# A graph layer on one core: edge matmuls on several partition bases, x in table order, spills by block, and the output's x part made ahead

## The chip, the core and the metric

The kernel runs on one core of a Trainium2 chip. The core has five engines that run side by side: TensorE (PE, with PEld for its weight loads), VectorE (DVE), ScalarE (ACT), GpSimd (POOL) and SyncE (SP). SP and ACT also issue ordinary DMA transfers, and POOL issues indirect ones (gathers). The metric is the time on the device in microseconds, from the first to the last instruction of a launch and what lies around it. The median of three runs before the change is 4903.21 us (4901.36 to 4903.9).

## The reference

There are 12,500 nodes with 96 features and 412,500 edges, sorted by destination; each has 4 attributes. Cut to what matters:

```python
def _mlp(h, W, b, gamma, beta):
    h = relu(h @ W + b)
    mu, var = mean(h, axis=0), mean(square(h - mu), axis=0)   # over all rows
    return gamma * (h - mu) * rsqrt(var + EPS) + beta

node_feat = _mlp(x, W_node, ...)                       # [12500, 96]
edge_feat = _mlp(edge_attr, W_edge, ...)               # [412500, 96]
message = concatenate([x[src], x[dst], edge_feat], 1)  # [412500, 288]
message = _mlp(message, W_msg, ...)
agg = segment_sum(message, dst, 12500)
out = layernorm(x + agg + node_feat)                   # each row
```

The three normalisations run over all nodes or all edges, so that the edge statistics must be complete before the first message can be formed, and the message statistics before the first output row.

## The kernel before

All numbers are float32. The message matmul is split: the products of x with the source part and with the destination part of W_msg are tables in DRAM, p_tab and q_tab, with a row for each node. Edges are worked in groups of 512 (GE), made of four tiles of 128 (GT = 4); four groups are a block (BG = 4). There are 806 groups and 202 blocks (NBL).

**Start.** `load_x` (L132) brings x, transposed to [96, 12544], in seven pieces on SP and ACT. `table` (L139) makes p_tab: one matmul for each of 98 blocks of 128 nodes, four to a PSUM tile, copies on DVE and ACT in turn, and a write for each four. Beside it, DVE computes each edge's place relative to its group's first destination (L163).

**Gathers.** `gather` (L261) issues one indirect DMA for each 128 edges; it brings 128 rows of p_tab by source (3223 in all). The first 104 groups (SPILL) are gathered and written to the DRAM tensor `spill` by SP (L272), group by group. The next 34 groups fill a ring of 34 tiles (RING). After that a gather waits until the message loop has used a tile.

**Nodes.** `nodes` (L178) makes q_tab, with all of its writes on ACT, the node branch's statistics (L187 to L189), and x plus the node branch in `agg`, which it writes to the DRAM tensor `xn_d` (L198). Then the space of x is given up.

**Edge statistics.** `edge_norm` (L200) loads the destinations, subtracts and writes `rel_d` (L208 to L212, two pieces). For each block it multiplies the 20 rows of edge attributes (4 groups x 5, the fifth row being ones) by three 128-column slices of the block-diagonal matrix `wide` (L221), applies Relu on ACT (L224) and takes statistics on DVE (L226). The attributes come from ACT's queue, four blocks to a load (J = 4), in three buffers.

**Messages.** The loop goes through the blocks in an order that mixes the 26 spilled blocks evenly among the others. `load` (L296) brings a block's attributes, relative destinations and rows of q_tab on SP. `prepare` (L310) makes four matmuls with 24 rows each (L316): the attributes and the relative destinations against `we`, whose four copies stand at different rows and are zero elsewhere. `message` (L320) multiplies per 128 edges (L324), adds the gathered rows (L330) and applies Relu (L331). `reduce` (L333) sums by destination with a matmul (L339) and adds to `agg` (L342) and to a Gram matrix for the message statistics (L343). `fetch` (L354) brings a spilled block back.

**Output.** After the message statistics, each block of 128 nodes gets two matmuls (L570 for the messages, L571 for the part from `xn_d`), statistics per row (L577, L578) and the scaling (L582), and is written out by SP (L585). `general` (L396) is for other inputs and isn't run here.

**What sets the order.** The source is traced once, and the framework's planner puts the instructions on the engines' queues. Among those whose inputs and buffers are there, by its own costs, it takes the one that comes first in the source; a later one can be placed ahead where an earlier one isn't ready. Each queue then runs strictly in that order. The transfers that SP and ACT issue take one of eight semaphores in turn, and a transfer waits for the one that had its semaphore before, whichever queue issued it. A pool that is opened after another has been closed takes its space, and waits for the tiles that lay there.

Of the kernel before, what the change touches and what calls it, by code (L numbers as in the profile page):

```python
# [22 lines left out]
P = 128  # L23
# [10 lines left out]
ER_ROWS = BG * (EK + 1)  # L34
# [6 lines left out]
NBK = 4  # L41

# [6 lines left out]
RING = 34  # L49
J = 4  # L50
# [14 lines left out]
def gnn(ctx, tc, t):  # L65
# [5 lines left out]
    xn_d = dram.tile([C, NN], F32, name="xn_d")  # L71
# [4 lines left out]
    vec = const.tile([C, len(_VECS)], F32, name="vec")  # L76
    w_node = const.tile([C, C], F32, name="w_node")
    w_msg = const.tile([C, 3, C], F32, name="w_msg")
    b_msg = const.tile([1, C], F32, name="b_msg")
    src = const.tile([P, NTP], I32, name="src")  # L80
    nc.sync.dma_start(w_msg, t["L0_gnn_W_msg"].rearrange("(s k) f -> k s f", k=C))
    nc.scalar.dma_start(src, t["src"])
    nc.scalar.dma_start(w_node, t["L0_gnn_W_node"])
    nc.scalar.dma_start(b_msg, t["L0_gnn_b_msg"])
    for i, name in enumerate(_VECS):
        nc.scalar.dma_start(vec[:, i:i + 1], t[name])
    v = {name[7:]: vec[:, i:i + 1] for i, name in enumerate(_VECS)}
# [10 lines left out]
    wide = const.tile([BG * EK, BG * C], F32, name="wide")  # L98
    we = const.tile([ER_ROWS, BG, C + WN], F32, name="we")
    step = const.tile([1, 2, WN], F32, name="step")  # L100
# [5 lines left out]
    for i in range(BG):  # L106
        k = EK * i
        for to in (wide[:, i * C:(i + 1) * C], we[:BG * EK, i, :C]):
            nc.scalar.dma_start(to[k:k + ED, :], t["L0_gnn_W_edge"])
            nc.scalar.dma_start(to[k + ED:k + EK, :], t["L0_gnn_b_edge"])  # L110
        nc.scalar.dma_start(we[k + ED:k + EK, i, C:], step[:, 0, :])
        nc.scalar.dma_start(we[BG * EK + i:BG * EK + i + 1, i, C:], step[:, 1, :])

    agg = const.tile([C + 1, NN], F32, name="agg")
    rel = const.tile([P, NGP, GT], F32, name="rel")
    base = const.tile([1, NGP], I32, name="base")
    mstat = const.tile([C, 2], F32, name="mstat")
    flag = const.tile([1, 1], I32, name="flag")
    nc.scalar.dma_start(base, t["base"])
# [12 lines left out]
    def load_x(pool):  # L132
        xt = pool.tile([C, NN], F32, name="xt")
        step = 14 * P
        for i, c in enumerate(range(0, NN, step)):
            (nc.sync if i % 2 == 0 else nc.scalar).dma_start(xt[:, c:c + step], t["x"][:, c:c + step])
        return xt

    def table(out, w, xt, work, ps, other=nc.sync):  # L139
        rows = out.rearrange("(b p) f -> p b f", p=P)  # L140
        for i in range(0, NB, NBK):
            n = min(NBK, NB - i)
            pt = ps.tile([P, NBK, C], F32, name="pt", bufs=3)
            for g in range(n):
                nc.tensor.matmul(pt[:, g, :], xt[:, (i + g) * P:(i + g + 1) * P], w, start=True, stop=True)  # L145
            r = work.tile([P, NBK, C], F32, name="trow", bufs=4)
            if (i // NBK) % 2:
                nc.scalar.activation(r[:, :n, :], pt[:, :n, :], AF.Copy)
            else:
                nc.vector.tensor_copy(r[:, :n, :], pt[:, :n, :])  # L150
            (other if (i // NBK) % 2 else nc.scalar).dma_start(rows[:, i:i + n, :], r[:, :n, :])

    rpool, xpool = ExitStack(), ExitStack()
    ring = rpool.enter_context(tc.tile_pool(name="ring", bufs=RING))
    xt = load_x(xpool.enter_context(tc.tile_pool(name="x", bufs=1)))
    with tc.tile_pool(name="win", bufs=1) as win, tc.tile_pool(name="win_w", bufs=2) as work, \
            tc.tile_pool(name="win_ps", bufs=2, space=PSUM) as ps:
        table(p_tab, w_msg[:, 0, :], xt, work, ps)
# [19 lines left out]
    def nodes(xt):  # L178

        with tc.tile_pool(name="nd", bufs=1) as one, tc.tile_pool(name="nd_w", bufs=2) as work, \  # L180
                tc.tile_pool(name="nd_ps", bufs=2, space=PSUM) as ps:
            table(q_tab, w_msg[:, 1, :], xt, work, ps, nc.scalar)
            stats = one.tile([C, -(-N // GE), 6], F32, name="nstats")
            for i, c in enumerate(range(0, N, GE)):
                n = min(GE, N - c)
                pn = ps.tile([C, GE], F32, name="pn")
                nc.tensor.matmul(pn[:, :n], w_node, xt[:, c:c + n], start=True, stop=True)  # L187
                nc.scalar.activation(agg[:C, c:c + n], pn[:, :n], AF.Relu, bias=v["b_node"], scale=1.0)
                nc.vector.bn_stats(stats[:, i, :], agg[:C, c:c + n])  # L189
# [4 lines left out]
            for c in range(0, NN, NN // 7):  # L194
                x, y = agg[:C, c:c + NN // 7], xt[:, c:c + NN // 7]
                nc.vector.scalar_tensor_tensor(x, x, a_n, y, op0=OP.mult, op1=OP.add)
                nc.vector.tensor_scalar(x, x, c_n, None, op0=OP.add)
                nc.scalar.dma_start(xn_d[:, c:c + NN // 7], x)  # L198

    def edge_norm():  # L200

        with tc.tile_pool(name="es", bufs=2) as work, tc.tile_pool(name="es1", bufs=1) as one, \
# [3 lines left out]
            for i in range(0, RW // GE, BG):  # L206
                lin = one.tile([EP // RW, BG, GE], I32, name="lin")
                nc.scalar.dma_start(lin, t["dlin"].rearrange("o (p g e) -> (o p) g e", g=RW // GE, e=GE)[:, i:i + BG, :])  # L208
                rlin = one.tile([EP // RW, BG, GE], F32, name="rlin")
                nc.vector.tensor_tensor(rlin, lin, first[:, i:i + BG].unsqueeze(2)  # L210
                                        .to_broadcast([EP // RW, BG, GE]), op=OP.subtract)
                nc.scalar.dma_start(rel_d.rearrange("o (p g e) -> (o p) g e", g=RW // GE, e=GE)[:, i:i + BG, :], rlin)  # L212
            stats = one.tile([P, NS, NBL, 6], F32, name="estats")
            for b in range(NBL):
                if b % J == 0:
                    ea = work.tile([BG * EK, J, GE], F32, name="ea", bufs=3)
                    n = min(J, NBL - b)
                    nc.scalar.dma_start(ea[:, :n, :], t["ea"][:, b:b + n, :])
                pr = ps.tile([P, NS, GE], F32, name="pr")
                for i in range(NS):  # L220
                    nc.tensor.matmul(pr[:, i, :], wide[:, i * P:(i + 1) * P], ea[:, b % J, :],  # L221
                                     start=True, stop=True)
# [37 lines left out]
    def fast(ring, xt):  # L260
        def gather(g):  # L261
            pg = ring.tile([P, GT, C], F32, name="pg")
# [7 lines left out]
        for g in range(SPILL):  # L270
            pg = gather(g)
            nc.sync.dma_start(spill[g // BG, :, g % BG, :], pg.rearrange("p a b -> p (a b)"))  # L272
        got = {g: gather(g) for g in range(SPILL, SPILL + RING)}

        nodes(xt)
        xpool.close()
        w_e, bias = edge_norm()

        with tc.tile_pool(name="fix", bufs=1) as fix, tc.tile_pool(name="msg", bufs=2) as work, \
                tc.tile_pool(name="msg_ps", bufs=2, space=PSUM) as ps:  # L280
            nc.vector.memset(agg, 0.0)
# [14 lines left out]
            def load(s, b):  # L296

                n = min(BG, NG - b * BG)
                ea = work.tile([ER_ROWS, GE], F32, name="ea")
                nc.sync.dma_start(ea[:BG * EK, :], t["ea"][:, b, :])  # L300
                nc.sync.dma_start(ea[BG * EK:, :], rel_d[:, b * BG * GE:(b + 1) * BG * GE]
# [8 lines left out]
            def prepare(s, b, ea):  # L310
# [4 lines left out]
                for i in range(n):  # L315
                    nc.tensor.matmul(pr[:, i, :], we[:, i, :], ea, start=True, stop=True)  # L316
# [48 lines left out]
            for s, b in enumerate(order):  # L365
# [4 lines left out]
                for g in range(b * BG, min((b + 1) * BG, NG)):  # L370
# [8 lines left out]
                    if g >= SPILL and ahead < NG:  # L379
                        got[ahead] = gather(ahead)  # L380
                        ahead += 1
# [14 lines left out]
    def general(w_e, bias):  # L396

        with tc.tile_pool(name="gd", bufs=1, space=DRAM) as gd, tc.tile_pool(name="gfix", bufs=1) as fix, \
# [41 lines left out]
            def message(n, gathered, ea, dstf, to_spare, c, nt, rows, stat):  # L440
# [3 lines left out]
                nc.tensor.matmul(pr[:, :m], we[:EK, 0, :C], ea, start=True, stop=True)  # L444
# [100 lines left out]
    w_e, bias = fast(ring, xt)  # L545
# [6 lines left out]
    with tc.tile_pool(name="fin", bufs=2) as work, tc.tile_pool(name="fin_ps", bufs=2, space=PSUM) as ps:  # L552
# [5 lines left out]
        nc.tensor.matmul(pd, l, ident[:C, :C], start=True, stop=True)  # L558
# [4 lines left out]
        for i in range(0, NB, NBK):  # L563
            n = min(NBK, NB - i)
            xn = work.tile([C, NBK * P], F32, name="xn", bufs=4)
            nc.scalar.dma_start(xn[:, :n * P], xn_d[:, i * P:(i + n) * P])
            py = ps.tile([P, NBK, C], F32, name="py", bufs=3)
            for g in range(n):
                b = i + g
                nc.tensor.matmul(py[:, g, :], agg[:, b * P:(b + 1) * P], d, start=True, stop=False)  # L570
                nc.tensor.matmul(py[:, g, :], xn[:, g * P:(g + 1) * P], ident[:C, :C], start=False, stop=True)  # L571
            st = work.tile([P, NBK, 6], F32, name="st", bufs=3)
            mv = work.tile([P, NBK, 2], F32, name="mv", bufs=3)
            sd = work.tile([P, NBK], F32, name="sd", bufs=3)
            y = work.tile([P, NBK, C], F32, name="y", bufs=4)
            for g in range(n):
                nc.vector.bn_stats(st[:, g, :], py[:, g, :])  # L577
                nc.vector.bn_aggr(mv[:, g, :], st[:, g, :])  # L578
            nc.scalar.activation(sd[:, :n], mv[:, :n, 1], AF.Sqrt, bias=eps, scale=1.0)
            nc.vector.reciprocal(sd[:, :n], sd[:, :n])  # L580
            for g in range(n):
                nc.vector.tensor_scalar(y[:, g, :], py[:, g, :], mv[:, g, 0:1], sd[:, g:g + 1],  # L582
# [39 lines left out]
```

## Time and profile before

| | us |
|---|---|
| median of 3 runs | 4903.21 |
| profiled execution | 4900.82 |
| its span, first to last instruction | 4899.1 |
| PE busy | 4229.2 (86%) |
| POOL busy | 3056.8 (62%) |
| DVE busy | 1845.6 (38%) |
| ACT busy | 1122.1 (23%) |
| mean granted TensorE clock | 0.708 |

The page lists each group of instructions with its line, engine, operation, what it writes and reads, how many there were, the busy time with the mean of one in ns, and the engine's idle time just before them with what ended most of it. The waits list who waited for whom: the total in us, how often, and the longest. In the timeline each row is a start, a duration, the instruction, and in brackets the idle time before it. In the table of stages each row is a stretch in us from the start with its length, then the busy time of each engine with its number of instructions, the granted clock, the DMA engines' busy share and GB/s. A matmul in float32 shows as two records.

### The profile page before, as it was taken

What the parts mean: (1) busy time and instruction counts of PE and PEld (TensorE: products, weight loads), DVE (VectorE), ACT (ScalarE), POOL (GpSimd) and SP (SyncE); (2) the same over time, 40 slices, a digit from 0 to 9 for tenths busy, and PEclk for the clock granted to TensorE, in tenths of its full rate; (3) what the DMA queues carried; (4) which work ended last, traced back from release to release, by engine and by line L of the source; (5) the groups of instructions that cost most, each with busy time, mean ns of one, the idle gap of its engine ahead of it and who ended that gap; (6) DMA issues with size and microseconds to landing.
All of it is one profiled execution on the core that took longest, in us unless ns stands there. A gap on an engine that the chain in (4) does not pass through costs nothing. (4 is left out here: it accounts for less than half of the span.)

```text
span 4899.1 us, 53507 instructions
## 1 busy us (share of the span) xinstructions
PE 4229.2 (86%) x16561; PEld 2777.4 (57%) x16561; DVE 1845.6 (38%) x4481; ACT 1122.1 (23%) x1289; POOL 3056.8 (62%) x3231
## 2 busy tenths in 40 slices
PE   7226999999979998888888888888888888888988
PEld 6102333333337776666666666666666666666667
DVE  2313333333345553333333333333333333333335
ACT  1102222222223332222222222222222222222220
POOL 2777772000007777777777777777777777777771
PEclk9655555555559997777777777777777777777775
DMA  5333210000002222222222122222222212222113
GB/s 162 114 105 100 86 50 24 8 8 8 8 20 61 55 55 52 53 52 52 52 52 52 45 53 52 52 52 52 52 52 53 52 45 52 52 52 52 46 45 87
DMA packets 213517, 266.70 MB, mean 54 GB/s; under 512 B 134615, under 2 KB 148023, under 8 KB 211564
## 3 DMA queue, kind: packets, MB, share of 16 engines
q0 software_dynamic: 103136, 158.62, 13.5%
q1 hardware_dynamic: 83212, 72.27, 4.9%
q10 hardware_dynamic: 26876, 32.28, 2.2%
q8 instruction: 137, 2.24, 0.2%
q14 instruction: 156, 1.28, 0.1%
HBM read 221.54 MB, written 41.35 MB: 54 GB/s over the span
## 5 line engine op out<-in xcount | busy, mean ns | idle before, releaser
L265 POOL DMA_INDIRECT pg<-p_tab,src x3223 | 3055.9, 948 | 1737.9 <-issue 866.2
L339 PE MATMUL pa<-h 128*97 128x127 f32 x6446 | 1066.1, 320 | 287.2 <-ACT h L331 282.3
L324 PEld LDWEIGHTS z<-rhs,left 127*128 127x128 f32 x6446 | 1030.9, 239 | 467.2 <-issue 244.1
L221 PE MATMUL pr<-ea,wide 20*128 20x512 f32 x1212 | 1035.3, 1053 | 207.3 <-DMA ea<-in_ea 144.6
L324 PE MATMUL z<-rhs,left 127*128 127x96 f32 x6446 | 1136.4, 326 | 72.5 <-DVE hs L330 68.0
L339 PEld LDWEIGHTS pa<-h 128*97 128x97 f32 x6446 | 926.6, 201 | 313.3 <-ACT h L331 304.3
L316 PE MATMUL pr<-ea,we 24*126 24x512 f32 x1612 | 1057.3, 788 | 14.0 <-DVE left L318 11.7
L330 DVE TENSOR_TENSOR hs<-z,pg 128x384 f32<-128x384 f32 x702 | 391.0, 557 | 1610.2 <-DMA pg<-p_tab,src 1066.4
L331 ACT ACTIVATE h<-hs 128x384 f32<-128x384 f32 x806 | 420.7, 522 | 2093.7 <-DVE hs L330 1384.1
L221 PEld LDWEIGHTS pr<-ea,wide 20*128 20x128 f32 x1212 | 396.1, 327 | 845.3 <-issue 779.4
L226 DVE BATCH_NORM_STATS2 estats<-r 128x6 f32<-128x512 f32 x606 | 379.3, 682 | 644.0 <-ACT r L224 644.0
L316 PEld LDWEIGHTS pr<-ea,we 24*126 24x126 f32 x1612 | 338.5, 230 | 379.7 <-issue 326.1
L224 ACT ACTIVATE r<-pr 128x1536 f32<-128x1536 f32 x202 | 292.8, 1450 | 948.7 <-PE pr L221 880.4
L317 ACT ACTIVATE left<-pr 96x2048 f32<-96x2048 f32 x202 | 376.9, 1866 | 476.9 <-PE pr L316 476.5
L318 DVE TENSOR_SCALAR left<-pr 30x2048 f32<-30x2048 f32 x202 | 462.8, 2291 | 16.5 <-ACT left L317 10.2
L342 DVE TENSOR_TENSOR agg<-pa,agg 97x30 f32 x806 | 149.2, 185 | 265.6 <-PE pa L339 261.9
L326 DVE TENSOR_TENSOR h<-rel,iota 128x120 f32<-128x120 f32 x806 | 205.1, 275 | 2.2
L343 DVE TENSOR_TENSOR gram<-pa,gram 97x97 f32<-97x97 f32 x806 | 202.1, 251 | 0.0
L330 DVE TENSOR_TENSOR hs<-z,pb 128x384 f32<-128x384 f32 x104 | 57.7, 554 | 164.5 <-PE z L324 163.4
L145 PE MATMUL pt<-w_msg,xt 96*128 96x96 f32 x392 | 86.7, 420 | 35.1 <-DMA xt<-in_x 32.8
L145 PEld LDWEIGHTS pt<-w_msg,xt 96*128 96x128 f32 x392 | 86.8, 333 | 47.7 <-DMA xt<-in_x 21.5
L570 PE MATMUL py<-dm,agg 97*128 97x96 f32 x196 | 62.0, 422 | 1.8 <-DVE y L582 1.5
(90 smaller groups left out, 440.8 us busy)
## 6 DMA issues: line engine op xcount, KB each, us to landing
pg<-p_tab,src POOLq DMA_INDIRECT x3223, 2.4
spill<-pg SPq DMA_DIRECT2D x104, 192.0 KB
pb<-spill SPq DMA_DIRECT2D x26, 768.0 KB
rhs<-q_tab SPq DMA_DIRECT2D x806, 11.2 KB
ea<-in_ea SPq DMA_DIRECT2D x202, 40.0 KB
ea<-in_ea ACTq DMA_DIRECT2D x50, 160.0 KB
xn_d<-agg ACTq DMA_DIRECT2D x7, 672.0 KB
q_tab<-trow ACTq DMA_DIRECT2D x24, 192.0 KB
```

Of the source, the lines that this page charges most:

```text
L221: nc.tensor.matmul(pr[:, i, :], wide[:, i * P:(i + 1) * P], ea[:, b % J, :], start=True, stop=True)
L224: nc.scalar.activation(r, pr, AF.Relu)
L226: nc.vector.bn_stats(stats[:, i, b, :], r[:, i, :])
L265: nc.gpsimd.indirect_dma_start(out=pg[:, i, :], out_offset=None, in_=p_tab[:, :], in_offset=bass.IndirectOffsetOnAxis(ap=src[:, k:k + 1], ...
L316: nc.tensor.matmul(pr[:, i, :], we[:, i, :], ea, start=True, stop=True)
L317: nc.scalar.activation(x[:C, :n, :], pr[:C, :n, :], AF.Relu)
L318: nc.vector.tensor_scalar(x[C:C + WN, :n, :], pr[C:, :n, :], 0.0, None, op0=OP.is_equal)
L324: nc.tensor.matmul(z[:, i, :], left[s % 2][:KR, g % BG, i * P:(i + 1) * P], rhs[:KR, s % 2, g % BG, :], start=True, stop=True)
L326: nc.vector.tensor_tensor(h[:, :, C + 1:C + 1 + WN], rel[:, g, :].unsqueeze(2).to_broadcast([P, GT, WN]), iota[:, None, :].to_broadcast([P ...
L330: nc.vector.tensor_add(hs[:, :n, :], z[:, :n, :], pg[:, :n, :])
L331: nc.scalar.activation(h[:, :n, :C], hs[:, :n, :], AF.Relu)
L339: nc.tensor.matmul(pa[:, :C + 1 + WN], h[:r, i, :C + 1], h[:r, i, :C + 1 + WN], start=i == 0, stop=i == n - 1)
```

## The change

- **x in table order.** x is loaded first, from a second copy in DRAM (`xp`) whose columns are permuted so that partition p of the table's blocks holds nodes 98 p to 98 p + 97. A table write is then 14 blocks (CH) with 5,376 contiguous bytes per partition. The small loads of weights follow the table, on SP, and are fewer. The writes of both tables alternate between SP and ACT.
- **Spills by block.** Four groups are gathered into one stage tile (two of them) and written at once; the ring has 30 tiles.
- **Several partition bases.** `wide` has three slices at partitions 0, 32 and 64, each with the 10 rows that its 128 columns need; the attributes are loaded to the same partitions (three loads for eight blocks, J = 8, two buffers). In the message loop the four groups' attributes stand at partitions 0, 32, 64 and 96 (from `eaq`, padded to 128 rows), and each matmul takes 6 rows of its own base.
- **The output's x part made ahead by node.** `nodes` runs after `edge_norm`, loads x once more, forms x plus the node branch in place, multiplies each block by a centring matrix (identity less 1/96), and writes the result by node to `y0_d`. The message part is centred in its own small matrix. The output then adds the two, squares, sums, and scales, for eight blocks at a time.
- q_tab is made before the statistics. The index part of `edge_norm` comes in four pieces instead of two.

```diff
-RING = 34
-J = 4
+RING = 30
+J = 8
+    def table(out, w, work, ps):
+        rows = out.rearrange("(p b) f -> p b f", b=NB)
+        for c in range(0, NB, CH):
+            r = work.tile([P, CH, C], F32, name="trow", bufs=3)
+            for j, i in enumerate(range(0, CH, NBK)):
...
+            (nc.scalar if c // CH % 2 else nc.sync).dma_start(rows[:, c:c + CH, :], r)
+    for i in range(NS):
+        k, n = Q * i, C - Q * i
+        nc.sync.dma_start(wide[k:k + EK, :n], t["wb"][:, C - n:])
+        nc.sync.dma_start(wide[k + EK:k + 2 * EK, n:], t["wb"][:, :P - n])
...
     def nodes():
+            xt = one.tile([C, NN], F32, name="xt")
+            for c in range(0, NN, NN // 7):
+                nc.scalar.dma_start(xt[:, c:c + NN // 7], t["x"][:, c:c + NN // 7])
...
-                nc.vector.scalar_tensor_tensor(x, x, a_n, y, op0=OP.mult, op1=OP.add)
-                nc.vector.tensor_scalar(x, x, c_n, None, op0=OP.add)
-                nc.scalar.dma_start(xn_d[:, c:c + NN // 7], x)
+                nc.vector.scalar_tensor_tensor(y, x, a_n, y, op0=OP.mult, op1=OP.add)
+                nc.scalar.activation(y, y, AF.Identity, bias=c_n, scale=1.0)
+            nc.vector.memset(agg, 0.0)
+            for i in range(0, NB, NBY):
+                n = min(NBY, NB - i)
+                py = ps.tile([P, 2, GE], F32, name="py0")
+                for g in range(n):
+                    nc.tensor.matmul(py[:, g // NBK, g % NBK * C:(g % NBK + 1) * C],
+                                     xt[:, (i + g) * P:(i + g + 1) * P], center, start=True, stop=True)
...
+                nc.scalar.dma_start(y0_d[i // NBY][:, :n * C], y0.rearrange("p a b -> p (a b)")[:, :n * C])
     def edge_norm():
-            for i in range(0, RW // GE, BG):
+            for i in range(0, RW // GE, 2):
...
-                    ea = work.tile([BG * EK, J, GE], F32, name="ea", bufs=3)
+                    ea = work.tile([P, J, GE], F32, name="ea")
                     n = min(J, NBL - b)
-                    nc.scalar.dma_start(ea[:, :n, :], t["ea"][:, b:b + n, :])
+                    for i in range(NS):
+                        nc.scalar.dma_start(ea[Q * i:Q * i + 2 * EK, :n, :],
+                                            t["ea"][EK * i:EK * (i + 2), b:b + n, :])
                 pr = ps.tile([P, NS, GE], F32, name="pr")
                 for i in range(NS):
-                    nc.tensor.matmul(pr[:, i, :], wide[:, i * P:(i + 1) * P], ea[:, b % J, :],
-                                     start=True, stop=True)
+                    nc.tensor.matmul(pr[:, i, :], wide[Q * i:Q * i + 2 * EK, :],
+                                     ea[Q * i:Q * i + 2 * EK, b % J, :], start=True, stop=True)
     def fast(ring):
-        for g in range(SPILL):
-            pg = gather(g)
-            nc.sync.dma_start(spill[g // BG, :, g % BG, :], pg.rearrange("p a b -> p (a b)"))
-        got = {g: gather(g) for g in range(SPILL, SPILL + RING)}
-        nodes(xt)
+        for b in range(SPILL // BG):
+            pg = ring.tile([P, BG, GT, C], F32, name="stage", bufs=2)
+            for i in range(BG):
+                gather(b * BG + i, pg[:, i, :, :])
+            nc.sync.dma_start(spill[b], pg.rearrange("p g a c -> p g (a c)"))
+        got = {g: ahead_of(g) for g in range(SPILL, SPILL + RING)}
+        with tc.tile_pool(name="tab_w", bufs=1) as work, tc.tile_pool(name="tab_ps", bufs=2, space=PSUM) as ps:
+            table(q_tab, w_msg[:, 1, :], work, ps)
         xpool.close()
         w_e, bias = edge_norm()
+        nodes()
             def load(s, b):
-                nc.sync.dma_start(ea[:BG * EK, :], t["ea"][:, b, :])
-                nc.sync.dma_start(ea[BG * EK:, :], rel_d[:, b * BG * GE:(b + 1) * BG * GE]
+                nc.sync.dma_start(ea, t["eaq"][:, b, :])
+                nc.sync.dma_start(ea[EK:P:Q, :], rel_d[:, b * BG * GE:(b + 1) * BG * GE]
...
-                    nc.tensor.matmul(pr[:, i, :], we[:, i, :], ea, start=True, stop=True)
+                    nc.tensor.matmul(pr[:, i, :], we[Q * i:Q * i + EK + 1, :],
+                                     ea[Q * i:Q * i + EK + 1, :], start=True, stop=True)
...
+            y0 = work.tile([P, NBY, C], F32, name="y0", bufs=6)
+            nc.scalar.dma_start(y0[:, :n, :], y0_d[i // NBY][:, :n * C].rearrange("p (b f) -> p b f", f=C))
...
-                nc.tensor.matmul(py[:, g, :], agg[:, b * P:(b + 1) * P], d, start=True, stop=False)
-                nc.tensor.matmul(py[:, g, :], xn[:, g * P:(g + 1) * P], ident[:C, :C], start=False, stop=True)
+                nc.tensor.matmul(py[:, g // NBK, g % NBK * C:(g % NBK + 1) * C],
+                                 agg[:, (i + g) * P:(i + g + 1) * P], d, start=True, stop=True)
...
+                nc.vector.tensor_add(x, py[:, :, :NBK * C], x)
...
+            nc.scalar.activation(sq[:, :n, :], y0[:, :n, :], AF.Square)
+            nc.vector.tensor_reduce(sd[:, :n], sq[:, :n, :], axis=AX.X, op=OP.add)
+            nc.scalar.activation(sd[:, :n], sd[:, :n], AF.Sqrt, bias=eps, scale=1.0 / C)
             nc.vector.reciprocal(sd[:, :n], sd[:, :n])
+            nc.vector.tensor_tensor(y[:, :n, :], y0[:, :n, :], sd[:, :n].unsqueeze(2).to_broadcast([P, n, C]), op=OP.mult)
```

## The prediction

> **What bounds the kernel now.** I read the page's table of groups first, then the waits, then the timeline where the waits pointed, then the busy times of stages. The table alone misleads: PE is busiest (86%), POOL only 62%.
>
> ```profile
> L265 POOL DMA_INDIRECT pg<-p_tab,src x3223 | 3055.9, 948 | 1737.9 <-issue 866.2
> L221 PE MATMUL pr<-ea,wide 20*128 20x512 f32 x1212 | 1035.3, 1053 | 207.3 <-DMA ea<-in_ea 144.6
> L226 DVE BATCH_NORM_STATS2 estats<-r 128x6 f32<-128x512 f32 x606 | 379.3, 682 | 644.0 <-ACT r L224 644.0
> ```
>
> Of POOL's idle 1737.9 us, 866.2 are "issue": about 0.30 us after each gather. A gather thus takes 0.948 + 0.30 = 1.25 us of POOL whatever else happens, and 3223 of them about 4020 us. The waits say where the rest went:
>
> ```profile
> POOL pg L265 <- DVE hs L330: 679.6, 10, 672.8
> PE pr L221 <- DMA ea<-in_ea: 144.6, 1, 144.6
> SPq L272 <- DMA rel_d<-rlin: 36.6, 1, 36.6
> ```
>
> One wait of 672.8 us: the ring of gathered groups is full and the message loop has not begun. The timeline has both of its ends, and the stage table what lies between:
>
> ```profile
> 80.92 1.10 POOL L265 DMA_INDIRECT pg<-p_tab,src  x1 [79.34 <-issue]
> ...
> 1454.20 0.94 POOL L265 DMA_INDIRECT pg<-p_tab,src  x1 [672.75 <-DVE hs L330]
> ```
>
> ```profile
> core 0: us, PE busy (x) PEld busy (x) DVE busy (x) ACT busy (x) POOL busy (x), PEclk, DMA share, GB/s
> ...
> 407.00:1420.00 1013.00, 1003.88 (x1176) 384.46 (x1176) 377.74 (x597) 285.66 (x198) 283.05 (x300) 0.50 0.11 32
> 1420.00:1454.00 34.00, 11.41 (x25) 5.90 (x26) 20.39 (x28) 2.17 (x2) 0.00 (x0) 0.50 0.15 51
> 1454.00:4806.00 3352.00, 2977.93 (x14489) 2196.58 (x14487) 1301.62 (x3433) 789.11 (x1008) 2523.30 (x2671) 0.78 0.21 51
> 4806.00:4899.00 93.00, 84.79 (x394) 84.07 (x394) 57.47 (x320) 7.43 (x25) 0.00 (x0) 0.50 0.38 104
> ```
>
> From 1454 to 4806, 2671 gathers in 3352 us are 1.25 us each: POOL sets the message loop, and PE has 374 us to spare in it. From 407 to 1420 PE sets the edge statistics, always at clock 0.50. From 4806 PE sets the output. So the time is: first gather 80.9; 552 gathers until the ring is full at 781.5; the wait of 672.8; the other gathers; the output. What shortens POOL's start, its wait or the output counts in full, and nothing else does.
>
> **Parts that act on the start.** x is loaded first, and in larger table writes (14 node blocks, 5.4 KB a row piece, in place of 384 B). Before, PE stood still from 18 to 39 us because the last three x pieces were issued on ACT behind some forty small ones. The first 12 us moved 256 GB/s; 4.8 MB of x at about 220 take 22 us, faster than PE consumes: 98 blocks x 2 records x 0.2145 us (132 records in 28.3 us at 49 us) = 42 us. First piece at about 8 us, end of PE at 50, copy 0.6 and the last 0.7 MB write some 6: the first gather at about 58, **23 us** earlier. The small loads now go by SP after the table; before them nothing waits but the statistics, at 125 us. A bound: 50 (writes free) to 75 (writes queued behind small loads).
>
> **Spills by block.** 26 writes in place of 104, through two stage buffers; the ring keeps 30 tiles. A stage takes 16 x 1.27 = 20 us of gathers, its write some 10 us, so POOL doesn't wait unless a write is held over 10 us. Such holds exist: the third wait above is a spill behind a transfer it has no data from, because the framework gives transfers eight semaphores in turn and each waits for its predecessor's. Worth perhaps 2 x 30 us, but only taken from POOL's later wait, so nothing as long as that exceeds it. The ring is now full after 416 + 120 = 536 gathers: 58 + 536 x 1.269 (700.6 us / 552) = **738**.
>
> **Edge statistics.** Three matmuls a block, each with 20 rows at base 0, become three with 10 rows at bases 0, 32 and 64. The trace has no matmul away from base 0. Bounds of a block: 5.12 us as now (6 records x 0.853), if nothing overlaps; 1.95 us if DVE limits it (3 BATCH_NORM_STATS2 in 1.88 us, and ACT 1.45). The Trainium skill (TensorE: Matmul & The Clock Gate, "Measured speedup vs the span model") gives 3.07 times for four 32-row tiles at 512 columns; three tiles would then give near 1.9 us, DVE's bound. Against this stands the row: x1212 records for 606 matmuls. A float32 matmul is two records on the same rows; if matmuls start in program order (as that page also has it), the second record of one can overlap only the first of the next, so three of six are saved: 3 x 0.853 = 2.56 us at clock 0.50, which 20 active rows never left before. I take **2.6 us**, nearer to the row than to the rule: 525 us for 202 blocks; by the rule 394.
>
> The beginning: q_tab needs PE another 42 us and then xt's space is free: about 125 us, against 407 before, when node statistics, xn_d's transfers (203 to 258) and two index loads (DVE waited for them 111 us) came first. These loads remain, four of half size: they take some 60 us from DVE (half of 111, rounded up). Unhindered, the statistics end at 125 + 60 + 525 = 710. But ACT's loads of edge attributes, three for 8 blocks now, share the eight semaphores with the spills, and the spills end only at 58 + 416 x 1.274 + 12 = 600. If the planner placed the loads among the spills as if a block took 5.12 us, the statistics are held to that pace until 600: (600 - 125) / 5.12 = 93 blocks, and about 10 more by buffers that are ahead; the 60 us are then hidden. The other 99 take 257: end at **857**. I take this: the semaphores are seen to bind in the trace, and a planner that knows of the overlap is not.
>
> **Nodes behind the statistics.** Before, they lay beside the spills for nothing. Now, after the statistics: xt is loaded again, on ACT (4.8 MB, 24 us, into the space that the edge loads had), 25 matmuls keep pace (+6), DVE has the edge aggregates before it (16.6), norm 4, first SCALAR_TENSOR_TENSOR 2.1 and ACT 1.7, then 98 centred matmuls at 0.427 = 42 us, under which the copies, memset (10.5) and y0 writes lie. That is about 85; then one block is prepared as between 1440 and 1454: 15-20 us. From the statistics' end to the first message: **105 us** (34 before; 80 to 140). First message at 857 + 105 = 962. POOL's wait: 962 - 738 = 224 in place of 672.8: **449 us** saved.
>
> **Message loop.** POOL still needs 1.25 us a gather. Its edge matmuls on four bases save PE 2 to 3 us a block, which is worth nothing behind POOL. The loads grow from 40 to 256 KB: 44 MB more in 3350 us, 13 GB/s beside 51; DMA share 0.21 leaves room. Per block PE had 3352 / 202 = 16.6 us. Against the change speaks the Trainium skill (TensorEngine Tiling, "Key Properties"): changing the tiling mode drains the engine. No row shows a drain here; two per block at 0.2 us (1.053 for an isolated record less 0.853) would be 81 us of PE's spare 374: nothing, by POOL's row; 81 us if that cover were gone.
>
> **Output.** One matmul a block in place of two: 98 x 0.427 = 42 us, not 84. DVE per 8 blocks: sum, reduce and product at about 0.96 (384 elements took 0.557) and 0.18: 3.05 x 12.25 = 37, just hidden under PE. 9.6 MB in 50 us need a DMA share of 0.38 x 93 / 52 = 0.68. Square might need a table load (1.28) each time it alternates with Sqrt: 0 to 33 us; I take 0, since Copy, Relu and Sqrt make only two loads now. 93 becomes 52: **41 us** saved.
>
> **Sum.** 4899.1 - 23 - 449 - 41 = 4386 in the span. The profiled execution took 4900.8, the median of the runs is 4903.2, 4 above the span: **4390**. In short, it is 3529 + the end of the statistics.
>
> **Rivals.**
> Statistics not paced, or full overlap (0.29): end at 710, time 4243; with 1.95 us a block they end before 633, POOL never waits, and 4166 is the floor. For it: 8 semaphores and two buffers give lead. Against: the two records of a matmul.
> No overlap (0.12): the slices run one after another. End 125 + 60 + 1034 = 1219, paced up to 1310: 4752 to 4843. For it: no row of the trace shows any overlap.
> Slower, one mechanism (0.05): matmuls of 6 rows one after another leave the clock low in the message loop, and PE becomes its bound. Cold, a block costs 4 x 3.51 + 6.8 = 20.9 us, warm 11.5. With the first message at 1324, more than 17.4 us a block (mean clock under 0.69, now 0.78) makes it slower; at 0.60, 19.0 us, it is 5214. Against: PE that is behind runs 128-row matmuls densely, and in such stretches (1500 to 1550) the clock is 0.83 to 1.00. With overlap, even all cold costs 18.3 a block: +343 us, 4733.
>
> **Numbers.** Likeliest 0.52, own range 4290 to 4490; the rivals 0.29, 0.12, 0.05; 0.02 that gains and losses meet within 0.2%, about what this measurement can tell from no change. The range is 4165 to 4700, leaving out the last three. Faster 0.93, same 0.02, slower 0.05.
>
> **What will show it.** First gather near 58 us; ACT's edge loads waiting for spills until 600, then one block of statistics each 2.6 us (5.1: no overlap; 1.95: full); xt's load after the statistics; one POOL wait of some 224 us; 1.25 us a gather after it; an output of 52 us. The prediction is wrong if a block is not near 2.6, if q_tab's writes on SP get behind spills (xt's space would stay taken), or if gathers in the loop slow down.

## The result and the profile after

The changed kernel takes 4425.6 us (median of four runs, 4425.0 to 4427.5) where the kernel before, beside it, takes 4902.9 (4901.4 to 4903.9): a ratio of 0.903, with an interval of 0.901 to 0.904. Forecast were 4390, with a range of 4165 to 4700. The profiled span is 4423.6 us. The total came out within 1%, but by luck: two steps of the sum behind it were wrong by 80 and 73 us in opposite directions, and nearly cancelled.

The groups of the changed kernel, from the page: engine, tiles and shapes, number, then busy time and mean ns of one, then idle time before them.

```profile
L283 POOL DMA_INDIRECT pg<-p_tab,src x2807 | 2651.8, 945 | 1130.3 <-issue 681.4
L349 PE MATMUL z<-rhs,left 127*128 127x96 f32 x6446 | 1212.3, 337 | 253.0 <-DVE hs L355 244.0
L240 PE MATMUL pr<-ea,wide 10*128 10x512 f32 x1212 | 384.7, 1096 | 336.6 <-ACT r L243 245.2
L340 PE MATMUL pr<-ea,we 6*126 6x512 f32 x1612 | 585.9, 879 | 49.4 <-DVE left L343 35.2
```

The statistics' matmuls (L240) have the same 1212 records as before, but their union is busy for 384.7 us and no longer 1035.3. The mean of one record has even grown, to 1096 ns: the records lie on top of each other. Its idle time is put down to ACT's Relu, but that is ten waits, the longest 79.8 us, in which ACT itself was held, as the waits below show.

The waits of the changed kernel (total, times, longest, in us):

```profile
POOL pg L283 <- DVE hs L355: 278.7, 14, 274.8
ACT r L243 <- DMA spill<-stage: 162.6, 6, 80.4
DVE rlin L227 <- DMA lin<-in_dlin: 152.1, 4, 43.6
```

POOL's one wait is 274.8 us in place of 672.8. The other two lines are what still keeps the statistics back: spills, and four loads of indices, for three of which DVE waits over 40 us each.

The busy times of its stages, one row for each stretch, of which the second and third are parts of the first (time from, to, length, then busy time and instructions of PE, weight loads, DVE, ACT and POOL, the granted clock, DMA share and GB/s):

```profile
300.00:450.00 150.00, 50.42 (x156) 14.14 (x156) 52.26 (x85) 37.63 (x26) 113.73 (x120) 1.00 0.35 98
330.00:400.00 70.00, 45.39 (x144) 12.61 (x138) 42.72 (x71) 32.05 (x23) 52.93 (x57) 1.00 0.37 97
400.00:450.00 50.00, 0.00 (x0) 0.00 (x0) 0.00 (x0) 0.00 (x0) 37.81 (x41) 1.00 0.29 87
450.00:600.00 150.00, 56.99 (x183) 16.68 (x186) 55.91 (x92) 45.14 (x32) 113.27 (x121) 1.00 0.35 90
600.00:650.00 50.00, 50.00 (x168) 13.91 (x162) 49.39 (x82) 39.04 (x28) 37.76 (x40) 1.00 0.35 73
865.00:1001.00 136.00, 71.83 (x270) 54.33 (x270) 80.81 (x81) 32.00 (x36) 0.00 (x0) 0.69 0.29 89
1001.00:4372.00 3371.00, 2711.53 (x14491) 2137.02 (x14490) 1290.22 (x3434) 779.21 (x1008) 2538.57 (x2687) 0.76 0.25 65
4372.00:4423.00 51.00, 42.23 (x197) 41.89 (x196) 34.08 (x53) 14.13 (x26) 0.00 (x0) 0.50 0.63 180
```

One Relu on ACT is one block of statistics. Between 300 and 600 us there are 26 + 32 = 58, on the mean one each 5.2 us, but not at an even pace: between 330 and 400 us there are 23, and between 400 and 450 none. From 600 on there are 28 in 50 us, one each 1.8 us, with DVE full (49.39 of 50). The message loop makes 2687 gathers in 3371 us, 1.255 each, exactly as before. The output takes 51 us.

Single instructions of the changed kernel, in order of time (start, duration, then in brackets the idle time before it and what ended it):

```profile
53.50 1.10 POOL L283 DMA_INDIRECT stage<-p_tab,src  x1 [51.92 <-DMA p_tab<-trow]
...
122.31 1.02 DVE L143 COPY trow<-pt 128x384 f32<-128x384 f32 x2 [31.33 <-DMA q_tab<-trow]
...
281.73 1.45 ACT L243 ACTIVATE r<-pr 128x1536 f32<-128x1536 f32 x1 [138.08 <-issue]
...
462.91 2.79 ACT L243 ACTIVATE r<-pr 128x1536 f32<-128x1536 f32 x2 [80.40 <-DMA spill<-stage]
...
864.01 1.28 ACT L121 ACT_TABLE_LOAD   x1
...
884.95 0.29 ACT L121 ACTIVATE norm_edge<-eaggr,eps 96x1 f32<-96x1 f32 x1 [19.65 <-DVE eaggr L269]
885.66 0.15 DVE L124 TENSOR_TENSOR norm_edge<-norm_edge,eaggr 96x1 f32<-96x1 f32 x1
885.97 3.52 ACTq L187 DMA_DIRECT2D xt<-in_x  x7
...
935.46 10.51 DVE L203 MEMSET agg<- 97x12544 f32 x1 [2.56 <-DMA y_d<-y0s]
946.84 31.89 PE L208 MATMUL py<-center,xt 96*128 96x96 f32 x148 [10.16 <-DVE y0s L212]
992.61 2.09 PE L340 MATMUL pr<-ea,we 6*126 6x512 f32 x8 [13.89 <-DMA ea<-rel_d]
...
994.81 1.87 ACT L342 ACTIVATE left<-pr 96x2048 f32<-96x2048 f32 x1 [60.96 <-DMA rhs<-q_tab]
```

The first gather is at 53.5. In between, on SP's queue alone, a write of q_tab stands behind three spills until 117.4, and DVE waits 31.33 us for it:

```profile
77.20 40.05 SPq L295 DMA_DIRECT2D spill<-stage  x3
117.41 0.34 SPq L144 DMA_DIRECT2D q_tab<-trow  x1
```

The first Relu of the statistics starts only at 281.7. At 462.9 the Relus go on after a hold of 80.40 us that is put down to a spill: ACT has issued its next load of attributes only at 462.5. The last Relu has ended at 864, where ACT turns to the edge norm. The second load of x is issued at 886.0, 22 us later, and the centred matmuls that follow it stand still for 10.16 us behind the clearing of agg. The last two lines are the best measure of overlap in this trace: eight records of four matmuls on four bases take 2.09 us, where eight records one after another took 7.16 us before (L316). PE's ends are modelled, but ACT begins to read all four results at 994.81, 2.20 us after the first record began.

### The profile page after: what moved, and what is told of

It is laid out like the page before. It is cut to its first block, busy times and chain, and to the rows that moved or that the text cites. A ratio compares the mean times of both kernels' runs of the same rounds, so it can differ in the third digit from the quotient of the medians.

```text
span 4423.6 us, 52945 instructions
## 1 busy us (share of the span) xinstructions
PE 3295.7 (75%) x16561; PEld 2425.7 (55%) x16561; DVE 1806.7 (41%) x4225; ACT 1131.1 (26%) x1301; POOL 3050.1 (69%) x3231
## 5 line engine op out<-in xcount | busy, mean ns | idle before, releaser
L283 POOL DMA_INDIRECT pg<-p_tab,src x2807 | 2651.8, 945 | 1130.3 <-issue 681.4
L364 PE MATMUL pa<-h 128*97 128x127 f32 x6446 | 1154.3, 338 | 367.6 <-ACT h L356 350.5
L349 PE MATMUL z<-rhs,left 127*128 127x96 f32 x6446 | 1212.3, 337 | 253.0 <-DVE hs L355 244.0
L240 PE MATMUL pr<-ea,wide 10*128 10x512 f32 x1212 | 384.7, 1096 | 336.6 <-ACT r L243 245.2
L340 PE MATMUL pr<-ea,we 6*126 6x512 f32 x1612 | 585.9, 879 | 49.4 <-DVE left L343 35.2
L283 POOL DMA_INDIRECT stage<-p_tab,src x416 | 397.4, 955 | 178.4 <-issue 126.5
L240 PEld LDWEIGHTS pr<-ea,wide 10*128 10x128 f32 x1212 | 108.3, 307 | 611.6 <-ACT r L243 509.2
L340 PEld LDWEIGHTS pr<-ea,we 6*126 6x126 f32 x1612 | 147.2, 237 | 122.6 <-DVE left L343 58.7
L351 DVE TENSOR_TENSOR h<-rel,iota 128x120 f32<-128x120 f32 x806 | 204.8, 275 | 2.1
L139 PE MATMUL pt<-w_msg,xp 96*128 96x96 f32 x392 | 85.0, 422 | 32.8 <-DVE trow L143 26.4
L139 PEld LDWEIGHTS pt<-w_msg,xp 96*128 96x128 f32 x392 | 84.0, 332 | 33.6 <-DVE trow L143 26.8
```

Of the source, the lines that this page charges most:

```text
L240: nc.tensor.matmul(pr[:, i, :], wide[Q * i:Q * i + 2 * EK, :], ea[Q * i:Q * i + 2 * EK, b % J, :], start=True, stop=True)
L283: nc.gpsimd.indirect_dma_start(out=pg[:, i, :], out_offset=None, in_=p_tab[:, :], in_offset=bass.IndirectOffsetOnAxis(ap=src[:, k:k + 1], ...
L340: nc.tensor.matmul(pr[:, i, :], we[Q * i:Q * i + EK + 1, :], ea[Q * i:Q * i + EK + 1, :], start=True, stop=True)
L349: nc.tensor.matmul(z[:, i, :], left[s % 2][:KR, g % BG, i * P:(i + 1) * P], rhs[:KR, s % 2, g % BG, :], start=True, stop=True)
L351: nc.vector.tensor_tensor(h[:, :, C + 1:C + 1 + WN], rel[:, g, :].unsqueeze(2).to_broadcast([P, GT, WN]), iota[:, None, :].to_broadcast([P ...
L364: nc.tensor.matmul(pa[:, :C + 1 + WN], h[:r, i, :C + 1], h[:r, i, :C + 1 + WN], start=i == 0, stop=i == n - 1)
```

## Experiments

The experiments ran on two other chips, which agree with each other and differ from the first: there the kernel before takes 6222 us, and the changed kernel 5738.8 (ratio 0.922, 0.919 to 0.924). The saving, 484 us, is close to that of the first chip (477), but the kernel before was not traced on these chips, so it is not shown that it is made up in the same way. Expected totals that were written for a chip like the first are therefore read as differences, against 5738.8 or against the run beside it. The edits are shown shortened.

**The changed kernel again.**

> The changed kernel itself, as the measure for the runs beside it. On a chip like the first: 4425 us, statistics held until about 600 us and ended near 864, POOL's wait 275 us. On a chip as slow as that of the earlier experiments (before: 6222 us there), near the 5733 us of the run with the split index transfers, or up to 40 us more, since that run took away the waits for indices.

Measured: 5738.8 us, within what was expected for such a chip. Its timeline in the statistics, with POOL's gathers left out:

```profile
607.61 1.45 ACT L243 ACTIVATE r<-pr 128x1536 f32<-128x1536 f32 x1 [14.65 <-remote]
...
609.12 2.08 PE L240 MATMUL pr<-ea,wide 10*128 10x512 f32 x6 [14.02 <-issue]
...
624.41 1.45 ACT L243 ACTIVATE r<-pr 128x1536 f32<-128x1536 f32 x1 [15.35 <-remote]
```

While POOL gathers, a block of statistics comes each 16.80 us here: PE has its six records done at 611.2, and ACT reads them at 624.4, though it has been idle for 15.35 us and its operands are there. When POOL's ring is full, at about 800 us, a block takes 1.84 us at once. On the first chip POOL gathered on from 600 to 726 us and the blocks took 1.86 beside it. What holds ACT on these chips is not in the records, and it stays open. The message loop is slower too: from 1400 to 5600 us there are 2611 gathers, one each 1.61 us, and POOL, which on the first chip set that loop at 1.255, now waits for DVE in it (637.4 us for L351). Three things follow. What is gained under POOL's gathers can hardly show here, so three of the experiments below (the index transfers alone, the three holds, the spills on POOL) are inconclusive. What sets the loop on the first chip can't be tested here either. And an isolated block is seen: **six records on three bases in 2.08 us**, where three matmuls one after another would be 5.12.

**Statistics slices back on base 0** (20 rows in every slice, the attributes loaded to partitions 0 to 19 only, one tile less in the ring).

```
-  matmul(pr[:, i, :], wide[Q*i:Q*i + 2*EK, :], ea[Q*i:Q*i + 2*EK, b % J, :])
+  matmul(pr[:, i, :], wide[:, i*P:(i + 1)*P], ea[:BG*EK, b % J, :])
```

> The changed kernel with its statistics slices put back to partition base 0 (20 rows each, three loads kept; ring 29 for space). If the gain comes from matmuls on different bases overlapping: a block of statistics takes 5.1 us again, about 150 blocks are left at 600 us, the statistics end near 1370, POOL's wait grows to some 780 us and the time is near 4930. If the gain comes from the earlier start and the other parts: a block stays under 3 us and the time within 20 us of 4425.

Measured: 6291.1 us, 552 more than the changed kernel on such a chip, and 1.1% more than the kernel before beside it (ratio 1.0108, interval 1.009 to 1.013). A window of this kernel, then one of the changed kernel in the same stage, in the columns given above, and POOL's longest wait for each:

```profile
1000.00:1200.00 200.00, 200.00 (x236) 78.11 (x235) 73.29 (x117) 56.55 (x39) 0.00 (x0) 1.00 0.03 8
```

```profile
900.00:1000.00 100.00, 100.00 (x327) 27.91 (x324) 98.70 (x163) 78.31 (x55) 0.00 (x0) 1.00 0.15 34
```

```profile
POOL pg L280 <- DVE hs L352: 1121.1, 31, 1030.7
```

```profile
POOL pg L283 <- DVE hs L355: 567.8, 33, 479.3
```

39 blocks in 200 us are 5.13 us each, against 55 in 100 us, 1.82: PE full in the one, PE and DVE in the other. POOL's wait grows by 551 us, the time by 552. So the partition bases are what the statistics owe their speed to, and the whole of it goes through POOL's wait. Without them the rest of the change gains nothing here: its nodes now stand between the statistics and the first message. The clock is granted at 1.00 in both, and a record at base 0 still takes 200 / 236 = 0.85 us, as it did at 0.50 before, on the first chip. The granted clock is therefore not what made the statistics fast.

**Edge matmuls of the loop back on base 0** (24 rows, with loads of 40 KB in place of 256; two tiles less in the ring).

```
-  matmul(pr[:, i, :], we[Q*i:Q*i + EK + 1, :], ea[Q*i:Q*i + EK + 1, :])
+  matmul(pr[:, i, :], we0[:, i, :], ea[:BG*(EK + 1), :])
```

> The changed kernel with the message loop's edge matmuls put back to base 0 (24 rows, 40 KB loads; ring 28 for space). If POOL sets the loop: PE's busy time in it grows by some 470 us (586 to 1057 for these matmuls), a gather stays at 1.255 us, and the time is 4425 within 10 us. If the bases matter in the loop (PE's clock or its drains): at least 40 us away from 4425, either way.

Measured: 5712.5 us, 0.5% under the changed kernel. Its group of these matmuls:

```profile
L346 PE MATMUL pr<-ea,we 24*126 24x512 f32 x1612 | 927.9, 700 | 140.2 <-issue 110.0 <-DVE left L348 19.7 <-DMA ea<-in_ea 10.4
```

PE is 325 us busier with them (927.9 against 602.8 in the changed kernel there; 470 was expected), and the kernel isn't slower for it. On these chips the loop isn't set by POOL alone, so this does not yet show what the bases are worth on the first. There the two traces show it: in the loop PE was busy for 2977.93 us before and for 2711.53 after, and a gather took 1.255 us both times. So the four bases are worth nothing in the loop, as forecast. Of a drain at each change of tiling no row shows a sign: in the changed kernel's trace PE's idle time before these matmuls is 49.4 us, of which 35.2 are put down to DVE, so drains on the way into them could be 14 us at most, as far as they show as idle time. The 26 us that this kernel is faster may be theirs, or those of the smaller loads: the run doesn't part them.

**Index transfers cut at partition 96.**

```
-  dma_start(lin, dlin[:, i:i + 2, :])
+  for lo, hi in ((0, 96), (96, 101)):
+      dma_start(lin[lo:hi], dlin[lo:hi, i:i + 2, :])        # rel_d likewise
```

> The changed kernel with each index transfer of 101 partitions cut into 96 and 5. If these transfers run on one DMA engine and hold the statistics until 281 us: each load takes under 20 us instead of 44, DVE's wait for them falls from 152 us to under 60, the first Relu comes before 220 us, some 15 more blocks are done by 600, and the time is near 4397. If the spills alone set the pace: the waits shrink and the time stays at 4425 within 8 us.

Measured: 5733.2 us, no difference from 5738.8. The waits for the loads shrank as expected: those that DVE's index subtraction has put down to them fall from 64.8 us to 5.1 (and those put down to nothing that the profile shows from 87.5 to 44.5), and the first Relu comes at 239 us in place of 342. But after it the statistics crawl at 16.8 us a block until POOL stops, and the last Relu comes at 1126 in place of 1138. What the 103 us would be worth on a chip like the first, this run can't tell.

**One spill in place of 26** (`SPILL = BG`). POOL's ring is full at 229 us, and after that neither gathers nor spills are left to disturb the statistics.

> The changed kernel with one spilled block instead of 26: nothing else moves, but POOL fills its ring by about 230 us and waits long, so it is slower as a whole. If the spills hold the statistics through the shared semaphores: these run at 1.86 us a block as soon as the index loads are over, end near 665 us, and the time is 665 + 137 + 3087 gathers at 1.255 + 52, some 4730. If something else holds them: they still end near 864 and the time is near 4930.

Measured: 5801.9 us. With the spills gone the statistics still got going only at 403 us, after two blocks at 371; from there they took 1.85 us a block and ended at 782. q_tab's copies had crawled until POOL stopped, and were done at 266; from there to 400 the four loads of indices followed one another. One row of its stage table, in which DVE, ACT and POOL stand almost still:

```profile
300.00:350.00 50.00, 3.78 (x4) 1.16 (x4) 1.23 (x1) 0.00 (x0) 0.00 (x0) 1.00 0.07 27
```

The DMA share is 0.07 of 16 engines, about what one engine can fill (an estimate: 1/16 is 0.06). The run after this one tests whether the cut changes that.

**One spill, and index transfers cut.**

> One spill only, and the index transfers cut at partition 96. With one spill and whole transfers the gathers had stopped at 229 us, no spill was left, and still the statistics got going only at 403 us, DVE waiting 124 us for four loads of indices. My theory (a transfer over 101 partitions is slow, and ACT's queue holds the attribute loads behind it): the four waits fall from 35 us to under 10 us each, the statistics get going about 100 us earlier, near 300 us, end near 680 in place of 782, and POOL's wait falls from 695 to about 595 us; the time falls by about 100 us. Rival (the indices wait for another reason, the shared eight semaphores or the q_tab writes): the four waits stay over 25 us each, and nothing moves by more than 20 us.

Measured: 5676.8 us, 125 less. The waits of the run with one spill, then of this one:

```profile
DVE rlin L227 <- DMA lin<-in_dlin: 123.7, 4, 35.2
...
POOL pg L283 <- DVE hs L355: 698.5, 2, 695.0
```

```profile
DVE rlin L228 <- DMA lin<-in_dlin: 18.4, 4, 6.9
...
POOL pg L285 <- DVE hs L357: 587.4, 4, 580.2
```

The waits for indices fall from 124 to 18 us; the statistics run from 295 us on and end at 668 in place of 780; POOL's wait is 115 us less. That is the theory's result, and the rival's (nothing moves by 20 us) is out. Uncut, DVE waits some 35 us for three of the four loads of 404 KB over 101 partitions (43 on the first chip), and ACT's queue holds the attribute loads and the Relus behind them. Cut into 96 and 5, a load keeps DVE waiting for less than 7 us; between 279 and 285 us, in the midst of them, the DMA share is 0.70. Loads and writes of the indices were cut together, so that their parts are not told apart.

**xt loaded by SP.**

```
-  nc.scalar.dma_start(xt[:, c:c + NN // 7], x[:, c:c + NN // 7])
+  nc.sync.dma_start(xt[:, c:c + NN // 7], x[:, c:c + NN // 7])
```

It was tried twice: alone, and on top of one spill and cut index transfers, where q_tab's writes were also put on ACT alone.

> Only the second loading of xt is issued by SP in place of ACT. My theory (the load stood in ACT's queue behind the edge norm's chain with its Sqrt): the load is issued within 3 us of the statistics' end, not 22 us after it; the first message comes about 20 us earlier, POOL's wait is 275 - 20 = 255 us and the time is 20 us less than the changed kernel's on the same chip. Rival (the nodes' stage is set by its memset, its y0 copies and its centred matmuls, and the load was covered): 0 to 5 us less.

> One spill only, index transfers cut at partition 96, q_tab written by ACT alone, xt loaded by SP. Against the run with one spill and cut transfers: xt's load is issued when the last statistics are done, not behind the edge norm's Sqrt (24 us later in the run with one spill), so the first message comes about 20 us earlier and POOL's wait is about 20 us less; the time falls by another 20 us. Rival (the nodes' stage is set by what follows the load): the first message comes less than 6 us earlier.

Measured: 5730.0 us for the first (0.9205 of before, interval 0.918 to 0.923: no difference from 0.9218), and 5676.8 for the second, the same as with one spill and cut transfers only. My theory, that the load stood in ACT's queue behind the Sqrt, fell. The timelines of the run with one spill and cut transfers, where ACT issues the load, and of the second of these, where SP does:

```profile
690.08 0.15 DVE L124 TENSOR_TENSOR norm_edge<-norm_edge,eaggr 96x1 f32<-96x1 f32 x1
...
690.38 3.64 ACTq L187 DMA_DIRECT2D xt<-in_x  x7
```

```profile
683.97 0.15 DVE L124 TENSOR_TENSOR norm_edge<-norm_edge,eaggr 96x1 f32<-96x1 f32 x1
...
684.25 3.37 SPq L187 DMA_DIRECT2D xt<-in_x  x7
```

SP's own wait in this run:

```profile
SPq L187 <- DVE norm_edge L124: 36.2, 1, 36.2
```

On either queue the load is issued 0.13 to 0.15 us after L124 has ended, 22 us after the last Relu, and the first message comes 139 us after that Relu in both. L124 is the last instruction that reads eaggr, a tile of the edge norm's own; xt is given the space that these tiles hold. The changed kernel's timeline shows the same order: ACT has done its Sqrt at 885.24 and would have been free, L124 ends at 885.81, the load is issued at 885.97. So the queue is not what holds the load: it waits for L124 on either. That it does so for the space is read from the traces and the program; a kernel that gives xt space of its own was not tried.

**Three holds taken away together** (indices, q_tab's writes all on ACT, xt by SP), and **the same with the spills issued by POOL** through three stage buffers, the ring cut to 25.

```
-  nc.sync.dma_start(spill[b], pg)
+  if b: nc.gpsimd.dma_start(spill[b - 1], held)
+  held = pg
```

> Three holds taken away together: index transfers cut at partition 96, q_tab written by ACT alone, xt loaded by SP. If the late indices and q_tab are what kept the statistics to 57 blocks by 600 us, then about 100 are done by then, the statistics end near 780 instead of 864, and with 20 us of the nodes the time is 100 us less than the changed kernel's. Rival (the spills alone set the pace until 600, whatever comes before them): the statistics still end at 850 to 864, and the time is 20 to 35 us less.

> The same three, and the spills are issued by POOL one stage later, through three stage buffers (the ring has 25 tiles in place of 30). If the statistics were held because loads on ACT and spills on SP wait for one another in turn, then they run at 1.86 us a block from about 190 us on and end by 600; POOL's wait falls from 275 us to less than 40, and the time is near 4200 us on a chip like the first (4166 was the floor worked out). Rival (the loads are late for another reason, the planner's order or the transfers themselves): the statistics still end after 780 and the time is within 40 us of the run with three holds taken away.

Measured: 5723.8 (0.9194, interval 0.917 to 0.922) and 5737.4 us (0.9214). Neither can be told from 0.9218, and both expectations of a gain are missed. With the spills on POOL, POOL gathered without a pause (121 gathers from 150 to 300 us, against 96 in the changed kernel on this chip), and the other engines got less done beside it: PE 48 records in that time, against 136, and the first Relu at 573 us, against 342. The statistics again ran at 1.84 us only when POOL had stopped, and ended near 1130 us in both. On these chips that is the bound, so whether spills on another queue would free the statistics on a chip like the first was not shown.

## Why the prediction was right, step by step

- **First gather**: forecast 58, measured 53.5. Ring full: forecast 738, measured 727. Both from the first load of x and 1.25 to 1.27 us a gather.
- **A block of statistics: the step that failed first.** I took 2.6 us, arguing from the row that two records of one float32 matmul can't overlap and that only the second of one matmul with the first of the next could. From 600 us on it is 1.86 us on the first chip, DVE's bound. The isolated block settles why: six records in 2.08 us. One matmul's two records are 1.71, so the three run side by side almost from end to end; three of six records saved, as I had it, would have left 2.56. The clock, which I took to stay at 0.50, was granted at 1.00, but that made no record faster (slices back on base 0). The factor of 3.07 in the Trainium skill (TensorE: Matmul & The Clock Gate, "Measured speedup vs the span model") would have come nearer: an estimate from it for four matmuls is 4 x 1.71 / 3.07 = 2.2 us, and the four of the message loop took 2.09. I set it aside for an argument that no row of the trace showed.
- **The beginning of the statistics: the step that failed second.** I let them start at 125 us, and hid the index loads, 60 us, behind the pace of the spills. The first Relu came at 281.7. Two holds stand there. q_tab's last copy was made at some 143 us, because its writes on SP queued behind spills (DVE and ACT waited 31 us each), a case that I had named as one that would break the forecast; its last write was done, and its space free, only at 162.4, as DVE's next instruction shows, which waited 18.42 us for it. And the index loads took DVE 152 us, not 60. My 60 was a slip in the sum: four loads of half the size are as many bytes as the two of before, for which DVE had waited 111, so there was nothing to halve. The runs with one spill show the cost of these loads by itself: 115 us of POOL's wait.
- **The pace until 600** was right as a mean: 58 blocks in 300 us are 5.2 us each, as if a block still cost 5.12. It was wrong as a picture: the blocks came in bursts at full speed, 23 of them between 330 and 400 us while spills went on, with holds between them, the longest 80.40 us, each put down to a spill that a load of attributes waited for. So spills held single loads, but they did not pace every block. Whether the mean comes out at 5.2 because the planner placed the loads for blocks of 5.12, as I had assumed, or by chance stays open: no run took the spills alone away on such a chip.
- **The statistics' end**: forecast 857, measured 864. By 600 us 60 blocks were done, not 103: 43 more behind it, at 1.86, cost 80 us. The 99 that I had counted there each took 0.74 less: 73 us gained. The two errors leave 7. So the right total is luck here. With the true cost of a block and my beginning it would have been 784.
- **The nodes, a term that was too small**: forecast 105 us from the statistics' end to the first message, measured 137. I let x be loaded from the first moment, with the edge norm's aggregates (16.6 us) under the load. It came 22 us later, since xt takes the space of tiles that the edge norm reads last. I let the clearing of agg lie under the centred matmuls; PE waited 10.16 us for it, and 4 for the first copy, and the matmuls took 57 us from first to last in place of 42. The rest was some 5 us shorter than I had it: 22 + 15 - 5 = 32.
- **POOL's wait**: forecast 224, measured 274.8, which is the 7 and the 32 above, and a ring full 11 us earlier. **Loop**: 1.255 us a gather, unchanged. **Output**: forecast 52, measured 51.
- **The sum**: 4386 was forecast for the span, 4423.6 was measured. The 37 us are 7 of the statistics, 32 of the nodes, and 1 back from the output, within a microsecond of rounding.

Of the rivals, no overlap at all and a cold message loop are out: the loop's clock was 0.76 and POOL set it. The rival of full overlap was right about the block and wrong about the total, because the statistics were held until 600 on the mean as in the likeliest case.

The version with one spill and cut index transfers is 62 us faster than the changed kernel on the chips of the experiments (5676.8 against 5738.8). It gives up POOL's lead: 3087 gathers are left for its loop. On a chip like the first, at 1.255 us each, from a first message at 807 and with an output of 51, this would be an estimated 4732 us, or some 120 less if q_tab is done by 143 us as in the changed kernel there, which is slower than 4425.6 either way; it was not run there.

## What to carry to other kernels

Cost a step that is split over partition bases by its isolated group: one row of six or eight records in 2 us is worth more than an argument on how records could pair up. And look at the rows within a mean before calling it a pace. When an edit speeds up a stage, look at what feeds it from the first microsecond: here DVE's waits for index transfers over 101 partitions, 111 us before and 152 after, came to stand beside matmuls of only 385 us. And before moving a load to another queue, compare its issue with the last reader of the space that it is to fill, since moving it gains nothing while it waits for that reader.

## What the runs showed of the hardware that was not expected

- Float32 matmuls of a few rows on three or four bases overlapped almost fully, both of their records: six records in 2.08 us and eight in 2.09, against 0.85 us for each record on one base.
- The pace of records on one base did not follow the granted clock: 0.85 us a record at a clock of 0.50 (the statistics before, on the first chip) and at 1.00 (slices back on base 0, on another).
- For loads of 404 KB over 101 partitions DVE waited 35 to 44 us each in three cases of four, with a DMA share of 0.07; cut into 96 and 5 partitions, its waits were under 7 us.
- On two chips, while POOL issued gathers, the other engines were held between instructions: a block of statistics each 16.80 us, against 1.84 as soon as POOL paused. On the first chip nothing of this was seen. The cause is open.
